# First chunk of a recurrent layer with experts: three sums per job read from the matmul bank by VectorE

## The chip, the cores and the metric

The kernel runs on one core of a Trainium2 chip, as one launch. The metric is the device time of the launch in microseconds. The core has five engines that run side by side and wait for each other by semaphores: TensorE (PE in the profile, its weight loads PEld), VectorE (DVE), ScalarE (ACT), GpSimd (POOL) and SyncE (SP), which issues most of the transfers. [...] The kernel before takes 4155.28 us, the median of three runs (4152.07 to 4155.88).

## What is computed

The input x has 8 x 1024 rows of 512 numbers in float32. The reference, cut to what matters here:

```python
xn = layernorm(x)
# recurrent part, Din = 1024
proj = xn @ W1 + b1
hidden, forget_gate, input_gate = split(proj, 3)
# a gated linear recurrence along the rows, computed with logarithms
out_h = ...
s = out_h @ W2 + b2
# expert part
shared = (silu(xn @ shared_gate_w) * (xn @ shared_up_w)) @ shared_down_w
e = argmax(xn @ gate_w)              # one of 32 experts for each row
xs = xn * sigmoid(max(xn @ gate_w))
routed = (silu(xs @ routed_gate_w[e]) * (xs @ routed_up_w[e])) @ routed_down_w[e]
out = x + s * silu(shared + routed)
```

## The kernel before, in words

The kernel works in two stages. The first makes the recurrent part and the shared expert for 16 chunks of 512 rows; the second (from about 2780 us on) makes the routed experts. The change lies in the first chunk of the first stage.

**Jobs and products.** A chunk has 20 jobs. A job makes one 256-wide slice of one projection: f, i or h (forget, input and hidden part of `proj`, slices 0 to 3) or g or u (gate and up projection of the shared expert). The order is `0fih 1fih 0gu 2fih 1gu 3fih 2gu 3gu` (JOBS, L542). Jobs are numbered on through the chunks, so job 20 is the first one of the second chunk. The first three jobs of the first chunk are plain products (`plain`, L851); all others multiply two 2x2 block matrices with seven products instead of eight, in the form with shared partial sums (`multiply`, L880). Each product P1 to P7 is two matmuls of 128x128 by 128x256. In the trace, in which a float32 matmul shows two records, a product is four records; products that follow each other without a wait start 0.86 us apart.

**Banks.** A job has three accumulators in PSUM. The chain bank b (three buffers) takes P1, P6, P7 and P4 in this order, each adding to what is there; after each of them the bank is read out, and only then may the next one of the chain begin. Bank c takes P5 and then P3 on top of it. Bank a takes P2. In the first chunk bank a is always the single buffer x0 and bank c goes round u0, u1 and x1 (L908). From the second chunk on a and c take turns with x0 and x1 (L906); the first c product of the second chunk, P5 of job 20, takes x0.

**Reading out.** ScalarE copies the bank to a part tile in SBUF, with the bias of the projection where one is due (L931 a plain copy, L933 a copy with a bias; g and u jobs have no bias and use L931 throughout). The part tiles are p1 (of P1), a (P2), p5 (P5), u2 (P6), c (P3) and u3 (P7), each with two buffers; the trace drops the numbers, so p1 and p5 both show as p, and u2 and u3 both as u. Three of the four quarters of the job's output are then sums of two parts: a + p1, c + u2 and u3 + p5 (L943, `join`). They are put into the queue one slot later, on VectorE; from the second chunk on the sum u3 + p5 is made by GpSimd. The fourth quarter is P4's copy itself.

**Order of the work.** The order on each engine is written out by hand in slots (`manual_schedule`; the loop over `now`, L1613). A slot holds one product, so a job has seven slots: P1 of job n, P4 of job n-2, P5 of n, P7 of n-1, P2 of n, P6 of n and P3, in the first chunk of job n-1 (ORDER, L962). Everything else is put down for a slot with `at`: loads of weights, the partial sums of weight blocks (GpSimd L788 to L792, VectorE L794), the partial sums of output weights (GpSimd, 1024 wide, L1123), and per slice the steps of the recurrence (class Cell): Abs, Exp and Ln on ScalarE (L983, L987, L991), a difference and two corrections on VectorE (L995, L999, L1003), sigmoids and Relu on ScalarE (L1006, L1010, L1013), a value and a product on VectorE (L1016, L1019) and two scans of 128x512 on VectorE (L1028). An engine takes its queue strictly in order. From the second chunk on, matmuls of the output projection (L1239) stand between the products.

Of the kernel before, what the change touches and what calls it, by code (L numbers as in the profile page):

```python
# [11 lines left out]
ALU = mybir.AluOpType  # L12
# [22 lines left out]
def tile_kernel(  # L35
# [45 lines left out]
    nc = tc.nc  # L81
# [27 lines left out]
    def work(name):  # L109
# [11 lines left out]
        out=upper, in_=ones, pattern=[[1, P]], compare_op=ALU.is_gt, fill=0.0,  # L121
# [429 lines left out]
    HT = T // 2  # L551
# [21 lines left out]
    now = 0  # L573
    steps = {}

    def at(slot, what, *args):
        assert slot >= now
        steps.setdefault(slot, []).append(lambda: what(*args))
# [194 lines left out]
    def blocks(n):  # L773
        w = natural[n]
        return [w[:, k : k + KQ, m : m + P] for m in (0, P) for k in (0, KQ)]
# [62 lines left out]
    outs, banks = {}, {}  # L838

    def out_of(n):  # L840
        c, q = divmod(n, JC)
        p, kind = JOBS[q]
        outs[n] = jp.tile([P, 2, T], FP, tag="out", name=f"{kind}{c}_{p}", bufs=7)
        return outs[n]

    def bias(n, block):
        p, kind = JOBS[n % JC]
        col = "hfi".index(kind) * NJ + 2 * p + block
        return vec[:, col : col + 1]
# [30 lines left out]
    def multiply(name, n):  # L880

        c = n // JC
        kind = JOBS[n % JC][1]
        A11, A12, A21, A22 = blocks(n)
        S = sums.get(n)
        b = xnTs[c]

        def B(k, m):
            return b[:, k * KQ : (k + 1) * KQ, m * HT : (m + 1) * HT]

        lhs, rhs, bank = {
            "P1": lambda: (A11, B(0, 0), "b"),
            "P2": lambda: (A12, B(1, 0), "a"),
            "P3": lambda: (S[:, 3], B(1, 1), "c"),
            "P4": lambda: (A22, tsum[c, 4], "b"),
            "P5": lambda: (S[:, 0], tsum[c, 1], "c"),
            "P6": lambda: (S[:, 1], tsum[c, 2], "b"),
            "P7": lambda: (S[:, 2], tsum[c, 3], "b"),
        }[name]()
        new = name in ("P1", "P2", "P5")  # L900
        if new:
            if bank == "b":
                ps = ps_b.tile([P, 512], FP, tag="b", name=f"b{n}")
            else:
                if n >= JC:
                    tag = f"x{(n + (bank == 'a')) % 2}"  # L906
                else:
                    tag = "x0" if bank == "a" else ("u0", "u1", "x1")[n % 3]  # L908
                if tag[0] == "u":
                    ps = ps_u.tile([P, 2, HC], FP, tag=tag, name=f"{bank}{n}")  # L910
                    ps = ps.rearrange("p q f -> p (q f)")
                else:
                    ps = ps_x.tile([P, 512], FP, tag=tag, name=f"{bank}{n}")
            banks[n, bank] = ps
        ps = banks[n, bank][:, :HT]
        for k in range(KQ):
            nc.tensor.matmul(  # L917
                ps, lhsT=lhs[:, k, :], rhs=rhs[:, k, :],
                start=(new and k == 0), stop=(k == KQ - 1),

                skip_group_check=True,
            )

        def part(tag, bufs):
            o = jp.tile([P, HT], FP, tag=tag, name=f"{tag}{n}", bufs=bufs)
            outs[n, tag] = o
            return o

        def evict(o, block):
            if block is None or kind in "gu":  # L930
                nc.scalar.copy(o, ps)  # L931
            else:
                nc.scalar.activation(o, ps, AF.Identity, bias=bias(n, block))  # L933

        if name == "P1":
            out_of(n)
            evict(part("p1", 2), 0)
            return
        o = outs[n]

        def join(eng, out, *tags):
            l, r = (outs.pop((n, tag)) for tag in tags)
            at(now + 1, lambda: eng.tensor_tensor(out, l, r, ALU.add))  # L943

        if name == "P2":
            evict(part("a", 2), None)
            join(nc.vector, o[:, 0, :HT], "a", "p1")
        elif name == "P5":
            evict(part("p5", 2), None)
        elif name == "P6":  # L950
            evict(part("u2", 2), 0)
        elif name == "P3":
            evict(part("c", 2), None)
            join(nc.vector, o[:, 0, HT:], "c", "u2")
        elif name == "P7":
            evict(part("u3", 2), 1)
            join(nc.gpsimd if c else nc.vector, o[:, 1, HT:], "u3", "p5")
        elif name == "P4":
            evict(o[:, 1, :HT], 1)
            natural.pop(n)  # L960
# [652 lines left out]
    for now in range(END):  # L1613
        job = now // 7
        name, back = ORDER[now % 7]
        if now < 7 * NPL:
            plain(job, now % 7)
        todo = (job - back,) if name != "P3" else (job - 1, job)
        for n in todo:
            late = name == "P3" and n < JC  # L1620
            if NPL <= n < NJOB and n == job - (1 if late else back):
                multiply(name, n)
        for step in steps.pop(now, ()):
            step()
        while filled < due(now):
            next(fill)
            filled += 1
# [112 lines left out]
    with tc.tile_pool(name="wo", bufs=3) as wo, tc.tile_pool(name="so", bufs=3) as so:  # L1740
        n = nc.values_load(
            nov[0:1, 0:1], min_val=0, max_val=MAXOV,
            skip_runtime_bounds_check_because="a sum of at most MAXOV comparisons of counts that sum to N",
        )
# [59 lines left out]
```

## Time and profile before

| what | value |
|---|---|
| median of three runs | 4155.28 us (4152.07 to 4155.88) |
| the profiled execution | 4155.68 us, its span 4153.9 us |
| mean granted clock of TensorE | 0.997 |
| busy: VectorE, ScalarE, GpSimd | 2257.2, 2113.6, 1391.7 us |
| sums of L943 in the first chunk | 51 on VectorE |
| products of L917 in the first chunk | from 39.25 us on |
| first matmul of the output projection (L1239) | 167.93 us |

The span runs from the first to the last instruction that the profiler saw; the run's time holds a little more. Busy time of an engine is the sum of its instructions. In a timeline a row gives start, duration, engine, line, operation, output<-inputs, and in brackets how long the engine stood idle before and whose work ended that. A wait row names the engine and tile that waited, then what it waited for, then total us, times and the longest.

### The profile page before, as it was taken

How to read it: one execution, taken by the hardware profiler on the slowest of the kernel's cores; microseconds unless marked ns; L12 is line 12 of the kernel's file. 1: busy time of each engine (PE TensorE's matmuls, PEld its weight loads, DVE VectorE, ACT ScalarE, POOL GpSimd, SP SyncE). 2: the span in 40 equal slices, each digit the busy share in tenths (PEclk: the TensorE clock that was granted, in tenths of full speed). 3: DMA queues.
4: the chain of work that ended last, by engine and by line, in shares of the span. 5: the costliest groups of instructions: out<-in, count | busy, mean ns of one | idle time of the engine just before them, and what ended most of it. 6: DMA issues, size and time to landing. Idle time of an engine off the chain costs nothing. (4 is left out here: it accounts for less than half of the span.)

```text
span 4153.9 us, 60141 instructions
## 1 busy us (share of the span) xinstructions
PE 4101.2 (99%) x21515; PEld 3635.9 (88%) x21515; DVE 2257.2 (54%) x3682; ACT 2113.6 (51%) x4031; POOL 1391.7 (34%) x1539
## 2 busy tenths in 40 slices
PE   7999999999999999999999999999999999999997
PEld 5788888888888888888888888887899999999997
DVE  6655555564555645556555566534555656666631
ACT  5666666666766667666676666731222222222210
POOL 5322111221112211212112122634555555555542
PEclk9999999999999999999999999999999999999999
DMA  8766666666666766667666665575777787888884
GB/s 277 238 220 222 208 221 204 217 223 216 216 206 210 228 218 216 211 200 227 220 213 217 203 221 183 183 236 180 212 227 233 219 243 232 247 250 234 245 260 118
DMA packets 557537, 909.30 MB, mean 219 GB/s; under 512 B 55404, under 2 KB 315404, under 8 KB 556980
## 3 DMA queue, kind: packets, MB, share of 16 engines
q1 hardware_dynamic: 510356, 816.23, 60.7%
q0 software_dynamic: 46880, 89.20, 8.8%
q8 instruction: 172, 2.82, 0.3%
q14 instruction: 129, 1.06, 0.1%
HBM read 786.82 MB, written 136.37 MB: 222 GB/s over the span
## 5 line engine op out<-in xcount | busy, mean ns | idle before, releaser
L917 PE MATMUL b<-t,sums 128*128 128x256 f32 x2536 | 653.9, 380 | 14.1 <-ACT u L933 6.5
L1239 PE MATMUL u<-wP,s 128*128 128x256 f32 x2032 | 598.0, 380 | 2.0 <-issue 2.0
L917 PEld LDWEIGHTS b<-t,sums 128*128 128x128 f32 x2536 | 480.8, 190 | 83.9 <-ACT u L933 8.9
L331 PE MATMUL acc<-e_h,e_wd 128*128 128x284 f32 (+26 forms) x2048 | 514.7, 394 | 0.0
L1239 PEld LDWEIGHTS u<-wP,s 128*128 128x128 f32 x2032 | 386.9, 191 | 56.9 <-issue 4.2
L331 PEld LDWEIGHTS acc<-e_h,e_wd 128*128 128x128 f32 x2048 | 373.6, 190 | 64.9
L252 POOL DMA_INDIRECT e_xs<-rec,fours x276 | 300.0, 1087 | 91.4 <-issue 87.7
L917 PE MATMUL b<-t,nat 128*128 128x256 f32 x1268 | 325.9, 379 | 4.6 <-ACT u L931 3.8
L917 PE MATMUL a<-xnT,nat 128*128 128x256 f32 x1268 | 326.8, 380 | 0.0
L917 PE MATMUL b<-xnT,nat 128*128 128x256 f32 x1268 | 325.4, 379 | 0.0
L917 PE MATMUL c<-t,sums 128*128 128x256 f32 x1268 | 325.4, 379 | 0.0
L917 PE MATMUL c<-xnT,sums 128*128 128x256 f32 x1268 | 325.2, 379 | 0.0
L933 ACT ACTIVATE u<-b,vec 128x256 f32<-128x256 f32 x378 | 179.8, 476 | 188.3 <-PE b L917 172.3
L917 PEld LDWEIGHTS b<-t,nat 128*128 128x128 f32 x1268 | 240.5, 190 | 39.1 <-ACT u L931 5.4
L917 PEld LDWEIGHTS a<-xnT,nat 128*128 128x128 f32 x1268 | 241.9, 191 | 33.2
L917 PEld LDWEIGHTS b<-xnT,nat 128*128 128x128 f32 x1268 | 240.9, 190 | 33.2 <-issue 0.5
L917 PEld LDWEIGHTS c<-xnT,sums 128*128 128x128 f32 x1268 | 241.0, 190 | 32.8
L917 PEld LDWEIGHTS c<-t,sums 128*128 128x128 f32 x1268 | 240.9, 190 | 32.8
L1239 PE MATMUL u<-wP,h 128*128 128x256 f32 x768 | 225.1, 379 | 0.0
L995 DVE TENSOR_TENSOR d<-d,m 128x1024 f32<-128x1024 f32 x64 | 87.7, 1370 | 239.8 <-ACT m L991 239.8
L1239 PE MATMUL u<-wP,sh 128*128 128x256 f32 x720 | 215.6, 381 | 0.0
L406 ACT COPY e_s<-e_b 128x284 f32<-128x284 f32 (+21 forms) x216 | 84.4, 391 | 239.8 <-PE e_b L397 239.8
(291 smaller groups left out, 7796.5 us busy)
## 6 DMA issues: line engine op xcount, KB each, us to landing
sums<-sdram SPq DMA_DIRECT2D x300, 512.0 KB, 4.6
nat<-in_L_attn_W_dram SPq DMA_DIRECT2D x192, 512.0 KB, 4.5
e_w<-L_ffn_routed_gate_w_dram SPq DMA_DIRECT2D x128, 512.0 KB, 4.6
e_w<-n_L_ffn_routed_up_w_dram SPq DMA_DIRECT2D x128, 512.0 KB, 8.6
e_wd<-L_ffn_routed_down_w_dram SPq DMA_DIRECT2D x32, 2048.0 KB, 10.9
wP<-tdram SPq DMA_DIRECT2D x127, 512.0 KB, 3.9
nat<-L_ffn_shared_gate_w_dram SPq DMA_DIRECT2D x64, 512.0 KB, 4.6
nat<-n_L_ffn_shared_up_w_dram SPq DMA_DIRECT2D x64, 512.0 KB, 4.2
```

What stands on the lines that cost most here:

```text
L252: nc.gpsimd.indirect_dma_start(out=self.xs[t][:, b, :], out_offset=None, in_=rec1.rearrange("n (a d) -> (n a) d", a=NA), in_offset=bass.In ...
L331: nc.tensor.matmul(accs[m][:, :W], lhsT=self.wd[:, j, m * P : (m + 1) * P], rhs=h[:, :W], start=(j == 0), stop=(j == NI - 1),)
L406: nc.scalar.copy(o[:, :W], ps[:, :W])
L917: nc.tensor.matmul(ps, lhsT=lhs[:, k, :], rhs=rhs[:, k, :], start=(new and k == 0), stop=(k == KQ - 1),  skip_group_check=True,)
L933: nc.scalar.activation(o, ps, AF.Identity, bias=bias(n, block))
L995: nc.vector.tensor_tensor(d, d, self.li, ALU.subtract)
L1239: nc.tensor.matmul(ps[:, q, :], lhsT=lhs[:, q * P : (q + 1) * P], rhs=w[:, p],  start=(q == 0 and p == 0 and name in ("P1", "P2", "P5")), ...
```

## The change

For the first chunk (c == 0) the second, third and seventh product are no longer copied to a part tile by ScalarE. VectorE makes the sum in one instruction, with one input in the bank (`ps`) and the other in the part tile that was there before: p1, u2 or p5. The bias that u3 carried goes into the copy of P5 instead. As before, the sum is put down one slot after its product. The branch for u3 + p5 is on GpSimd in all other chunks, as it was.

```diff
+        def direct(out, tag):
+            r = outs.pop((n, tag))
+            at(now + 1, lambda: nc.vector.tensor_tensor(out, ps, r, ALU.add))
+
-        if name == "P2":
+        if c == 0 and name in ("P2", "P3", "P7"):
+            direct(*{
+                "P2": (o[:, 0, :HT], "p1"), "P3": (o[:, 0, HT:], "u2"), "P7": (o[:, 1, HT:], "p5"),
+            }[name])
+        elif name == "P2":
             evict(part("a", 2), None)
             join(nc.vector, o[:, 0, :HT], "a", "p1")
         elif name == "P5":
-            evict(part("p5", 2), None)
+            evict(part("p5", 2), None if c else 1)
...
         elif name == "P7":
             evict(part("u3", 2), 1)
-            join(nc.gpsimd if c else nc.vector, o[:, 1, HT:], "u3", "p5")
+            join(nc.gpsimd, o[:, 1, HT:], "u3", "p5")
```

## The prediction

> **What bounds the kernel.** I read the busy table first, then the windows, then what TensorE waited for, then the timelines of the stretch with idle time.
>
> ```profile
> PE 4101.2 (99%) x21515; PEld 3635.9 (88%) x21515; DVE 2257.2 (54%) x3682; ACT 2113.6 (51%) x4031; POOL 1391.7 (34%) x1539
> ```
>
> TensorE is busy 4101.2 of 4153.9 us, so whatever makes it wait is paid in full, and what any other engine saves is worth nothing unless TensorE waited for it. The chunk that the change touches runs from 39 to about 165 us. Its windows (stretch, length, busy time of TensorE, weight load, VectorE, ScalarE, GpSimd, granted clock, DMA):
>
> ```profile
> 60.00:70.00 10.00, 9.03 (x43) 7.62 (x42) 10.00 (x9) 9.95 (x17) 10.00 (x9) 1.00 0.90 317
> 70.00:80.00 10.00, 4.50 (x17) 3.28 (x16) 9.93 (x10) 4.99 (x10) 9.43 (x7) 0.91 1.00 369
> 130.00:140.00 10.00, 8.22 (x41) 5.95 (x40) 9.93 (x12) 2.19 (x6) 9.69 (x9) 1.00 0.45 152
> ```
>
> Summed from 40 to 165 us TensorE is idle 17.5 us; from 200 to 2300 us it shows none. So 17.5 us (0.42%) is all that this change can win. Look at the third busy column: VectorE is at 9.9 to 10 of 10 where TensorE idles most. The waits, TensorE's and then ScalarE's, in that stretch (total, times, longest):
>
> ```profile
> PE b L917 <- ACT u L931: 10.2, 7, 4.3
> PE b L917 <- ACT u L933: 7.3, 7, 2.1
> ```
> ```profile
> ACT u L933 <- DVE f L943: 10.4, 2, 5.3
> ACT u L931 <- DVE h L943: 4.6, 1, 4.6
> ```
>
> TensorE waits only for ScalarE's copies out of the chain bank. But three of these waits, TensorE's 4.28, 2.08 and 1.78 us, come after ScalarE itself stood still behind a VectorE sum that had yet to free its buffer. So 8.1 us are VectorE's doing and 9.3 us ScalarE's own queue: copies that stand behind table loads (1.28 us) and 1024-wide activations (1.06 to 1.15 us).
>
> **What is removed.** Jobs 3 to 19, 17 of them, lose three copies each: 51 ScalarE instructions. Copies of a and c show 376 and 374 ns and start 0.26 us apart when queued, biased ones 480 ns and 0.37 us apart. A job loses 0.26+0.26 and 0.26 (g, u) or 0.37 (f, i, h): about 0.83 us, or 14 us over the chunk. All of it lies beside TensorE work except where a copy of the chain bank stands behind it. P5's copy gets a bias for the 9 jobs of f, i, h: 480 against 381 ns, 0.9 us in all, beside other work.
>
> **What is changed on VectorE.** The same 51 sums stand at the same places in its queue (the seventh product's was VectorE's in this chunk already). Only the source changes. No row shows a 256-wide sum out of a bank, so I bound it. A 512-wide one with one input in a bank (L1251) takes 688 ns, and one with both in SBUF (L829) 690 to 699 ns: no extra. So an undisturbed 256-wide one should cost what the undisturbed SBUF one costs, 0.42 us; the other end is today's, 0.94 us where GpSimd works at the same time. These groups show which it will be:
>
> ```profile
> L943 DVE TENSOR_TENSOR f<-a,p 128x256 f32<-128x256 f32 x63 | 39.2, 622 | 120.6 <-ACT a L931 120.6
> L1222 DVE TENSOR_TENSOR a<-u,b2b 128x512 f32<-128x512 f32 x32 | 22.0, 688 | 33.9 <-PE u L1239 33.8
> L1251 DVE TENSOR_TENSOR o<-u,a 128x512 f32<-128x512 f32 x32 | 22.0, 688 | 20.5 <-PE u L1239 15.2 <-DMA rec<-o 5.2
> ```
>
> The 622 ns of the first is a mixture of 0.42 and 0.95; the two with a bank as source keep 688 ns in the mean, also where GpSimd works. I take 0.42 us. From 50 to 140 us that takes some 8 us off the stretched sums, but part comes back, since the next instruction with two SBUF inputs then waits for the same GpSimd instruction.
>
> [...]
>
> **What is added: TensorE now waits for VectorE's queue.** ScalarE used to empty bank a and the chain bank within about a microsecond or two. Now the next P2 needs the sum of this P2 (a single bank x0), P4 needs the P7 sum of its job, and P5 three jobs on needs the P3 sum. Behind the waiting product stands all of TensorE's queue. Where VectorE is late today, two buffers of each part hide it; this cover goes. TensorE, with the products P4, P5 and P7 of jobs 6, 8 and 7, and then VectorE:
>
> ```profile
> 72.46 1.13 PE L917 MATMUL b<-t,nat 128*128 128x256 f32 x4 [1.23 <-ACT u L931]
> 73.42 1.03 PE L917 MATMUL c<-t,sums 128*128 128x256 f32 x4
> 78.73 2.07 PE L917 MATMUL b<-t,sums 128*128 128x256 f32 x4 [4.28 <-ACT u L931]
> ```
> ```profile
> 74.01 3.41 DVE L1028 TENSOR_TENSOR_SCAN h<-i,ginit,f 128x512 f32<-128x512 f32 x1
> ...
> 77.52 0.69 DVE L943 TENSOR_TENSOR h<-c,u 128x256 f32<-128x256 f32 x1
> ...
> 79.00 0.94 DVE L943 TENSOR_TENSOR g<-u,p 128x256 f32<-128x256 f32 x1
> ```
>
> P4 of job 6 starts at 72.46, but the sum that it will need (g<-u,p) ends at 79.94: 7.5 us late. The same subtraction gives 6.0 us for job 9 (97.34 against 103.36) and 7.1 us for job 14 (133.21 against 140.36), and 1.3 to 5.6 us for ten others. These do not add up: VectorE's time sets them, and two products later stands a wait that TensorE has today anyway. With P4 at 80.0, P7 of job 7 follows two products (1.73 us) later at 81.7 and not 78.7: 3.0 us lost, not 7.5. Job 9 gives 103.4+1.7=105.1 against 101.3, 3.8 us; job 14 gives 140.4+1.7=142.1 against 136.9, 5.2 us, all if VectorE is as late as today. The next waits of today (1.18, 0.79 and 1.51 us) then swallow 3.5 us of it.
>
> **The sum is set at the last gate.** P5 of job 20 opens the next chunk, takes bank x0, and so must wait for the sum of job 19's P2. Past it ScalarE copies again, and TensorE has no wait that gives anything back. VectorE, TensorE and ScalarE:
>
> ```profile
> 170.49 0.98 DVE L943 TENSOR_TENSOR u<-a,p 128x256 f32<-128x256 f32 x1
> ```
> ```profile
> 166.21 1.03 PE L917 MATMUL c<-t,sums 128*128 128x256 f32 x4
> ```
> ```profile
> 160.60 1.08 ACT L1013 ACTIVATE h<-h 128x1024 f32<-128x1024 f32 x1
> ```
>
> - Upper end: that sum ends where it does now, 171.47. Then P5 is 171.47-166.21 = 5.3 us late, and 6.6 us if TensorE's lag costs ScalarE another 1.3 us.
> - Middle: VectorE last rests before 161.72, for the ScalarE instruction that ends at 161.68. From there to 171.47 it works without a gap, less 0.56 us for the one stretched sum: 9.2 us. ScalarE is busy from 140.44 up to its end but for 1.57 us (a wait for VectorE, which moves along), and loses eight copies in it, one at 0.37 and seven at 0.26 us, 2.2 us in all. So 161.68-2.2+9.2 = 168.7: P5 is late by 2.5 us. Two or three late P4 before it wake ScalarE late, 0.5 to 1 us: 3 us.
> - Lower end: VectorE also reaches 140 us earlier, by part of the 8 us. At 5 us the gate is open at 163.7 and TensorE, with the ScalarE waits of 9.3 us partly gone and P4's partly come, gains about 2 us.
>
> I take the middle: **4155.7 + 3 = 4158.7 us**. The profiled execution took 4155.68 us (1.8 beside its span of 4153.9), 0.4 above the median 4155.28 of the runs shown. About 0.2%, 8.3 us, is what a measurement of this kernel can tell from no change.
>
> **Rivals.**
> - *ScalarE's relief wins (faster).* The eleven waits that stem from ScalarE's own queue shrink (9.3 us), and sums at 0.42 us let VectorE run ahead, so that the three of 8.1 us shrink too. With two thirds of 17.5 us gone: 4144; the least that counts is 8.3 us. For it: 14 us of copies gone from a queue that TensorE waits for. Against: P6's copy, for which P7 waits 12.9 of the 17.5 us, stays on ScalarE.
> - *VectorE's backlog becomes the bound (slower).* The 8 us come back at the next two-input instructions, GpSimd's 2.3 us sums (L1123) hold the scans as today, and TensorE's lag delays ScalarE and so VectorE. It decides from the point where the sum of job 19's P2 ends after 166.2+8.3 = 174.5, 3 us later than now. Price 8.3 to 12: about 4166. The clock can add: after waits of 4.28 and 2.08 us the granted clock is 0.56 and 0.66 in the next 3.5 and 5 us, so a dip costs 3.5x0.44 = 1.5 to 5x0.34 = 1.7 us.
> - *It doesn't do what it says.* The built order shows 51 ScalarE instructions fewer and VectorE's in the same order; I give this nothing.
>
> [...]
>
> **Chances.** Forecast (within 8.3 us) 0.60, backlog 0.27, relief 0.13. For 8 in 10 the range leaves out the far parts of both rivals: 4148 to 4168. The forecast's own range, from the lower and upper ends, is 4153.5 to 4162.5.
>
> **What would show it.** Right: sums at 0.42 us throughout the chunk; ScalarE's copies of a and c gone before 165 us; TensorE's waits in the chunk for VectorE (L943's new line) on P4 of jobs 6, 9 and 14 at 2 to 5 us and on the first c product of the next chunk; first product of L1239, at 167.93 today, at about 171. Wrong: no TensorE wait for VectorE in the chunk (relief), or sums from a bank at 0.9 us (backlog), or a difference that arises after 200 us.

## The result, and the profile after

| | before | after |
|---|---|---|
| median (lowest to highest), 16 runs each | 4154.66 us (4151.96 to 4156.48) | 4162.09 us (4159.09 to 4166.63) |
| ratio after / before | | 1.0019, 95% interval 1.0012 to 1.0026 |
| the profiled execution, its span | 4155.68, 4153.9 us | 4163.02, 4161.3 us |
| chunk: first L917 product to first output product | 128.68 us | 137.64 us |
| TensorE idle in it | 17.48 us | 18.23 us |
| time at half the granted clock in it | 6.83 us | 27.31 us |

The change costs 7.4 us (0.19%); 4158.7 was forecast, so the sign was right and the size too small. The last three rows are worked out from the trace's records. They carry the explanation: TensorE waits about as long as before in sum, but four times as much time passes at half clock. (The profile records the clock that TensorE was granted; in every profile here it is either full, 1.00, or half, 0.50. A stretch at half clock is called a drop below.) In line numbers of the new kernel the sum from a bank is L947, the output product L1247, and what stood behind L943 has moved down by 8.

Busy time on the page of the new kernel, and the same three windows as before (stretch, length, TensorE, weight load, VectorE, ScalarE, GpSimd, clock, DMA share, GB/s):

```profile
PE 4107.3 (99%) x21515; PEld 3647.2 (88%) x21515; DVE 2248.9 (54%) x3682; ACT 2099.4 (50%) x3980; POOL 1394.9 (34%) x1539
```
```profile
60.00:70.00 10.00, 5.57 (x20) 4.47 (x21) 9.85 (x12) 6.50 (x10) 10.00 (x9) 0.88 0.59 229
70.00:80.00 10.00, 10.00 (x38) 8.42 (x37) 9.42 (x11) 6.14 (x10) 9.43 (x7) 0.78 0.71 243
130.00:140.00 10.00, 6.53 (x24) 5.21 (x23) 9.97 (x14) 1.21 (x3) 9.06 (x9) 0.79 0.37 117
```

ScalarE has 51 instructions and 14.2 us less. TensorE is "busy" 6.1 us more with the same number of matmuls, which is the mark of a slower clock, not of more work. From 70 to 80 us it looks fully busy (10.00), but the clock column shows 0.78: a busy share alone would call this stretch the best of the three.

The longest rows of what TensorE waited for from 40 to 180 us, and ScalarE's first row of waits for VectorE (total, times, longest):

```profile
PE b L917 <- DVE i L947: 6.8, 2, 3.5
PE b L917 <- DVE h L947: 3.0, 1, 3.0
PE b L917 <- DVE g L947: 2.9, 2, 2.2
PE a L917 <- DVE h L947: 1.7, 1, 1.7
PE c L917 <- DVE u L947: 1.6, 1, 1.6
PE b L917 <- ACT u L933: 0.9, 2, 0.8
```
```profile
ACT u L933 <- DVE f L947: 8.0, 2, 4.4
```

The waits for ScalarE, 17.5 us before, are down to 0.9; VectorE's sums have taken their place. Each long one is at P4, which needs the P7 sum of its job out of the chain bank: 3.00 us (job 5), 3.37 (job 9), 3.47 (job 14), 2.23 (job 16). What follows such a wait is seen in TensorE's timeline at P4 of job 5 and of job 14:

```profile
68.16 2.08 PE L917 MATMUL b<-t,nat 128*128 128x256 f32 x4 [3.00 <-DVE h L947]
70.02 1.92 PE L917 MATMUL c<-t,sums 128*128 128x256 f32 x4
```
```profile
137.11 2.08 PE L917 MATMUL b<-t,nat 128*128 128x256 f32 x4 [3.47 <-DVE i L947]
138.98 1.92 PE L917 MATMUL c<-t,sums 128*128 128x256 f32 x4
140.68 1.92 PE L917 MATMUL b<-t,sums 128*128 128x256 f32 x4
142.39 1.15 PE L917 MATMUL a<-xnT,nat 128*128 128x256 f32 x4
143.46 1.07 PE L668 MATMUL lgp<-xnT,gw 128*32 128x512 f32 x8
```

A product of four records takes 1.03 us at full clock; here four of them take 1.92 to 2.08 us and start 1.7 to 1.9 us apart instead of 0.86. The rows carry no mark for this: one sees it only by comparing durations of equal shape. The product of the router's logits (lgp) at the end starts at 143.46 instead of 138.80 us, and with it the rest of the chunk: ScalarE's copy of lgp stands in its queue ahead of the functions that VectorE needs. Before, TensorE's row of lgp and ScalarE's copy were:

```profile
138.80 1.07 PE L668 MATMUL lgp<-xnT,gw 128*32 128x512 f32 x8
```
```profile
142.28 0.61 ACT L673 COPY lgT<-lgp 128x512 f32<-128x512 f32 x1
```

After, ScalarE, then VectorE, then TensorE, to the end of the chunk:

```profile
144.60 0.59 ACT L673 COPY lgT<-lgp 128x512 f32<-128x512 f32 x1 [2.30 <-PE lgp L668]
...
157.93 0.37 ACT L931 COPY g<-b 128x256 f32<-128x256 f32 x1 [3.28 <-PE b L917]
...
163.09 1.06 ACT L1021 ACTIVATE h<-h 128x1024 f32<-128x1024 f32 x1
```
```profile
164.18 1.22 DVE L1024 SCALAR_TENSOR_TENSOR h<-m,h 128x1024 f32<-128x1024 f32 x1 [1.86 <-ACT h L1021]
...
172.95 0.41 DVE L947 TENSOR_TENSOR u<-a,p 128x256 f32<-128x256 f32 x1
```
```profile
173.42 2.07 PE L917 MATMUL c<-t,sums 128*128 128x256 f32 x4 [1.58 <-DVE u L947]
...
176.88 0.60 PE L1247 MATMUL u<-wP,h 128*128 128x256 f32 x2
```

The last gate exists: P5 of job 20 waits 1.58 us for the sum of job 19's P2, starts 7.2 us later than before, and at half clock; the first output product comes 9.0 us later (176.88 against 167.93). From 180 to 2300 us the clock is 1.00 and TensorE is full (2120.00 of 2120 us busy) in both kernels. One half-clock window of before at 2778 us (1.7 us of time) is absent in the profile after: 9.0 - 1.7 = 7.3, which is the difference of the two profiled executions.

### The profile page after: what moved, and what is told of

Same layout as the page of the kernel before. It is cut to its first block, busy times and chain, and to the rows that moved or that the text cites. A ratio compares the mean times of both kernels' runs of the same rounds, so it can differ in the third digit from the quotient of the medians.

```text
span 4161.3 us, 60091 instructions
## 1 busy us (share of the span) xinstructions
PE 4107.3 (99%) x21515; PEld 3647.2 (88%) x21515; DVE 2248.9 (54%) x3682; ACT 2099.4 (50%) x3980; POOL 1394.9 (34%) x1539
## 5 line engine op out<-in xcount | busy, mean ns | idle before, releaser
L917 PE MATMUL b<-t,sums 128*128 128x256 f32 x2536 | 655.2, 381 | 2.1 <-DVE t L829 1.2
L1247 PE MATMUL u<-wP,s 128*128 128x256 f32 x2032 | 596.8, 380 | 2.2 <-issue 2.2
L917 PEld LDWEIGHTS b<-t,sums 128*128 128x128 f32 x2536 | 484.1, 191 | 69.1 <-ACT u L933 1.8
L1247 PEld LDWEIGHTS u<-wP,s 128*128 128x128 f32 x2032 | 386.6, 190 | 55.7 <-issue 4.5
L917 PE MATMUL b<-t,nat 128*128 128x256 f32 x1268 | 329.9, 383 | 13.5 <-DVE i L947 6.8
L917 PE MATMUL c<-t,sums 128*128 128x256 f32 x1268 | 330.2, 384 | 1.6 <-DVE u L947 1.6
L917 PE MATMUL a<-xnT,nat 128*128 128x256 f32 x1268 | 326.5, 380 | 1.7 <-DVE h L947 1.7
L917 PE MATMUL b<-xnT,nat 128*128 128x256 f32 x1268 | 325.7, 379 | 0.4 <-DMA nat<-L_ffn_shared_gate_w_dram 0.4
L917 PE MATMUL c<-xnT,sums 128*128 128x256 f32 x1268 | 325.4, 379 | 0.0
L917 PEld LDWEIGHTS b<-t,nat 128*128 128x128 f32 x1268 | 242.7, 192 | 48.7 <-DVE i L947 7.6
L917 PEld LDWEIGHTS c<-t,sums 128*128 128x128 f32 x1268 | 244.2, 193 | 35.3 <-DVE u L947 2.0
L917 PEld LDWEIGHTS a<-xnT,nat 128*128 128x128 f32 x1268 | 242.3, 191 | 34.8 <-DVE h L947 2.1
L917 PEld LDWEIGHTS b<-xnT,nat 128*128 128x128 f32 x1268 | 241.4, 190 | 33.4 <-issue 1.3
L917 PEld LDWEIGHTS c<-xnT,sums 128*128 128x128 f32 x1268 | 241.4, 190 | 32.2
L1247 PE MATMUL u<-wP,h 128*128 128x256 f32 x768 | 225.4, 379 | 0.0
L1247 PE MATMUL u<-wP,sh 128*128 128x256 f32 x720 | 215.8, 381 | 0.0
```

Of the source, the lines that this page charges most:

```text
L917: nc.tensor.matmul(ps, lhsT=lhs[:, k, :], rhs=rhs[:, k, :], start=(new and k == 0), stop=(k == KQ - 1),  skip_group_check=True,)
L1247: nc.tensor.matmul(ps[:, q, :], lhsT=lhs[:, q * P : (q + 1) * P], rhs=w[:, p],  start=(q == 0 and p == 0 and name in ("P1", "P2", "P5")), ...
```

## The experiments

Three theories were put to the test. **A**: the sums that free the chain bank (P7) make TensorE wait for VectorE's queue, and that is the loss. **B**: not the waits cost, which sum up as before, but the half clock behind the long ones. **C**: the gate at the end of the chunk, where a bank passes to the next stage, sets the time. Each kernel's ratio is to the kernel before on the same chip in the same session (its median 4154.0 to 4154.8 us). "Up to lgp" is the time from the first L917 product to the logits' product (99.55 us before, 104.23 after), "from lgp" that from there to the first output product (29.13 and 33.41).

### One part at a time

P7 back on ScalarE, P2 and P3 direct:

```diff
-        if c == 0 and name in ("P2", "P3", "P7"):
+        if c == 0 and name in ("P2", "P3"):
...
-            evict(part("p5", 2), None if c else 1)
+            evict(part("p5", 2), None)
...
-            join(nc.gpsimd, o[:, 1, HT:], "u3", "p5")
+            join(nc.gpsimd if c else nc.vector, o[:, 1, HT:], "u3", "p5")
```

> The second and third product are still summed from the bank; the seventh goes back to ScalarE's copy and the sum of two part tiles, and P5's copy loses its bias again. Theory A (the chain bank is the gate: P4 waits for the P7 sum in VectorE's queue): the five waits of P4 for VectorE (3.0, 3.4, 0.7, 3.5, 2.2 us) and the half-clock stretches behind them go; 4151 to 4157 us, no slower than the kernel before. Theory C (the last gate sets the time: P5 of job 20 in bank x0 waits for the sum of P2 of job 19): this gate stays and VectorE's queue is as long, so 4159 to 4162.

Measured: 4158.2 us, ratio 1.0007 (0.9998 to 1.0016). Up to lgp 99.20 us, as before; from lgp 33.97, as after. The time lies between the two forecasts. About half of the loss goes with P7, as A says, and the profile shows the other half at the end of the chunk; the interval of what is left just reaches no change.

Only P7 direct:

```diff
+        if c == 0 and name == "P7":
```

> Only the seventh product is summed from the bank; second and third are copied by ScalarE as in the kernel before. Theory A: P4 waits for VectorE as in the changed kernel, 4159 to 4164 us. Theory C: the gate of bank x0 is gone with P2's sum, so 4153 to 4157.

Measured: 4165.9 us, 1.0027 (1.0017 to 1.0037): by the medians worse than all three together, though the intervals overlap. Its waits at P4 are 4.6, 3.6 and 4.8 us, up to lgp it takes 108.68 us, and from there 29.49, without a loss. Its rows of sums, the first two from SBUF, the third from the bank, say why:

```profile
L943 DVE TENSOR_TENSOR g<-a,p 128x256 f32<-128x256 f32 x4 | 3.6, 894 | 1.2 <-ACT a L931 1.2
...
L943 DVE TENSOR_TENSOR i<-a,p 128x256 f32<-128x256 f32 x3 | 1.8, 607 | 4.8 <-ACT a L931 4.8
...
L947 DVE TENSOR_TENSOR g<-b,p 128x256 f32<-128x256 f32 x4 | 1.7, 415 | 0.0
```

The other sums are stretched as before, so VectorE should reach the P7 sum later: it seems that the direct P2 and P3 sums help the third one to be on time.

Only P3 direct, and only P2 direct (the same line with `name == "P3"` and `name == "P2"`; P7 and P5 as in the kernel before):

> Only the third product is summed from the bank. Its bank comes round three jobs later, so its gate seldom closes. Theory A (the gate on a bank that is needed soon, with the half clock behind it, is the cost): no wait of TensorE for VectorE over 2 us, and ScalarE has 17 copies less: 4150 to 4156 us. If VectorE reading a bank is the cost as such: about a third of the change, 4156 to 4158.

Measured: 4161.15 us, 1.0016 (1.0007 to 1.0025). A miss for A. Up to lgp it is 98.27 us, but from lgp 34.52, and TensorE's timeline shows where:

```profile
166.07 1.03 PE L917 MATMUL b<-t,sums 128*128 128x256 f32 x4
172.85 1.22 PE L1247 MATMUL u<-wP,h 128*128 128x256 f32 x2 [5.75 <-DVE g L947]
```

The output projection's first product takes over bank u0, and in u0 stands the c sum of job 18, which VectorE now empties. A second gate at the end, that the prediction had not seen.

> Only the second product is summed from the bank. Theory A: P2 of the next job waits for VectorE where it is late, above all job 7 (about 4.8 us, as with P2 and P3 together) and P5 of job 20 (4.3 us), with half clock behind both: 4156 to 4161 us. If the third product's sum made the loss of the run with P2 and P3 together: 4153 to 4156.

Measured: 4159.7 us, 1.0011 (1.0002 to 1.0020). Up to lgp 99.55 us, to the digit that of before, although P2 of job 7 waits 4.82 us in it and a drop of 6.8 us follows, so that the equality to the digit is chance; from lgp 33.60, with a wait of 4.31 us at P5 of job 20. What P2 alone costs shows at x0, at the end of the chunk.

### The clock

The new kernel with five matmuls that feed nothing, ahead of P4 of jobs 5, 9 and 14:

```diff
+                if name == "P4" and n in (5, 9, 14):
+                    idle = work(f"idle{n}")
+                    for _ in range(5):
+                        nc.tensor.matmul(
+                            idle[:, :HT], lhsT=ident, rhs=xnTs[0][:, 0, :HT], start=True, stop=True
+                        )
```

> The changed kernel with five matmuls more (128x128 by 128x256, result never read) ahead of P4 of jobs 5, 9 and 14, 2.2 us each time, in waits of 3.0, 3.4 and 3.5 us. Theory B (the waits themselves cost no more than before, the half clock behind the longer ones does): the three half-clock stretches of 6.8 us behind these waits go, and the time falls by 2 to 6 us to 4156 to 4160 though TensorE does more. If only the waits count: no change, 4161 to 4164, for the added work lies in the waits.

Measured: 4157.64 us, 1.0007 (0.9998 to 1.0016): 6.5 us of additional TensorE work make the kernel 4.5 us faster than the new kernel, and the slowest of its 11 runs (4159.09) is level with the fastest of the new kernel's 16. TensorE at P4 of job 5, and the window from 60 to 80 us (clock 0.83 in the kernel after):

```profile
64.99 2.32 PE L1633 MATMUL idle<-xnT,ident 128*128 128x256 f32 x10
68.16 1.13 PE L917 MATMUL b<-t,nat 128*128 128x256 f32 x4 [0.84 <-DVE h L947]
69.12 1.03 PE L917 MATMUL c<-t,sums 128*128 128x256 f32 x4
```
```profile
60.00:80.00 20.00, 17.59 (x79) 14.88 (x80) 19.78 (x22) 13.78 (x20) 19.77 (x15) 1.00 0.75 266
```

P4 starts at 68.16 us in both kernels, since VectorE sets that; but behind it the products take 1.03 us and not 1.92. B holds: up to lgp 99.12 us instead of 104.23.

The same in the kernel before, five ahead of P7 of job 7 and two ahead of P7 of job 10:

> The kernel before with five idle matmuls ahead of P7 of job 7 and two ahead of P7 of job 10 (waits of 4.28 and 2.08 us, each with 3.4 us of half clock behind it). Theory B: both half-clock stretches go, 1.7 us each, of which later waits of ScalarE's and VectorE's may swallow some: 1 to 3 us less than before, 4151 to 4153.5. If the half clock is no cost here: 4154 to 4156, as the kernel before.

Measured: 4154.61 us, 1.0000 (0.9991 to 1.0009). A miss: no gain. The two drops of the clock went, but a wait of 2.9 us arose at 88 us, with a drop of its own.

Where do the drops come from? In all fourteen profiles the edges of the half-clock times stand on a grid of 3.413 us (in the profile before, half-clock times begin at 78.186 and 2778.128 us, and the 2699.942 us between them are 791 steps of 3.4133). Counted over the chunk (in the one profile without a drop there, the grid is read from the half-clock time at the end of the kernel): every full-clock grid window with 2.02 us or more of TensorE idle time is followed by one at half clock (34 of 34), and none with 1.71 us or less; of the seven in between, 1.72 to 1.84 us, one is. A half-clock window with 0.63 us idle or more is followed by another (10 of 10), one with 0.58 us or less is not. So the place of a wait in the grid should count, not its length alone. Two and four such matmuls ahead of job 3, the first one with seven products, shift all waits against the grid:

```diff
+                if name == "P1" and n == 3:
+                    idle = work(f"idle{n}")
+                    for _ in range(2):
```

> The changed kernel with two idle matmuls (0.87 us) ahead of the chunk's first job, so that all its waits come 0.87 us later in the program. In every profile so far the drops of the clock stand on a grid of 3.413 us that is nearly fixed against the start of the program, and a grid window with 2.02 us or more of TensorE idle time is followed by one at half rate, one with 1.74 us or less is not. Theory 'the grid': the waits of 3.0, 3.4, 2.2 and 1.6 us are now cut in two by a window's edge, their windows hold 1.5 to 1.65 us each, and only the wait at P4 of job 14 keeps a drop: half-clock time falls from 27.3 to 3.4-7 us, 10 to 12 us of time at half rate less 0.9 us; since the grid moves by some 0.5 us from one execution to the next, the median should gain part of it: 4153 to 4158.5 us. Theory 'a long wait brings its drop wherever it stands': the same drops and 0.9 us more, 4163 us (4161 to 4165).

Measured: 4159.84 us, 1.0014 (1.0005 to 1.0023). TensorE at P4 of job 5, the same wait as after:

```profile
68.88 1.13 PE L917 MATMUL b<-t,nat 128*128 128x256 f32 x4 [3.01 <-DVE h L947]
69.84 1.03 PE L917 MATMUL c<-t,sums 128*128 128x256 f32 x4
```

A wait of 3.01 us, cut by an edge into 1.36 and 1.64, and no drop. The half-clock time in the chunk is 6.83 us instead of 27.31, as the grid says; but the time lies between the two forecasts of this run, outside both. Idle time rose from 18.23 to 21.92 us: part of what the slow clock had taken would have been waited for VectorE anyway.

> The changed kernel with four idle matmuls (1.73 us) ahead of the chunk's first job. Theory 'the grid': windows at P4 of jobs 5, 9 and 14 hold 2.35 to 3.0 us of idle time and little follows in the next, so each brings one drop of 3.4 us and not 6.8, and those at 156 and 173 us go: 10.2 us at half rate in place of 27.3, 8.5 us less, and 1.7 us more work: 4155.3 us (4154 to 4159), more than with two idle matmuls. Theory 'a long wait brings its drop wherever it stands': 4163.8 us (4162 to 4166).

Measured: 4160.68 us, 1.0017 (1.0008 to 1.0026). Five drops of 3.41 us, 17.06 in all: the three at P4 are single as forecast, the two at the end did not go, and the time is again outside both forecasts. The edges themselves lay up to 1.7 us apart against the chunk's start from one execution to the next, which is half a window; a shift of the program does not control them.

### The last gate

From the second chunk on, banks x0 and x1 exchanged, with P7 direct and with P7 back:

```diff
-                    tag = f"x{(n + (bank == 'a')) % 2}"
+                    tag = f"x{(n + (bank != 'a')) % 2}"
```

> The changed kernel with the banks x0 and x1 exchanged from the second chunk on, so that P5 of job 20 takes x1 and need not wait for the sum of P2 of job 19. Theory C: the wait of 1.6 us and the half clock of 3.4 us behind it go, 3.3 us less: 4158 to 4159.5. If VectorE's lateness is merely met at another place (P2 of job 20 in x0, four slots and the first matmuls of the output projection later): 4160 to 4163.

Measured: 4160.78 us, 1.0014 (1.0005 to 1.0023).

> Second and third product from the bank, the seventh by ScalarE, and the banks x0 and x1 exchanged from the second chunk on. Of the run without the exchange (4158.2) the last gate took 4.3 us and two half-clock stretches (6.8 us, 3.4 lost). P2 of job 20 meets the same sum some 3.5 us later, so 2 to 5 us less: 4153 to 4156. If the gate is merely met later at its full price: 4157 to 4159.

Measured: 4159.39 us, 1.0015 (1.0006 to 1.0024), a miss. In both the wait at P5 of job 20 is gone, and the first output product waits instead, 2.4 and 5.2 us, for the sum in u0. Opening one gate only brought the other to light.

Both gates at once: jobs 17 to 19 are copied by ScalarE as before, all others stay direct. Then the same with the fillers:

```diff
-        if c == 0 and name in ("P2", "P3", "P7"):
+        if n < 17 and name in ("P2", "P3", "P7"):
...
-            evict(part("p5", 2), None if c else 1)
+            evict(part("p5", 2), 1 if n < 17 else None)
...
-            join(nc.gpsimd, o[:, 1, HT:], "u3", "p5")
+            join(nc.gpsimd if c else nc.vector, o[:, 1, HT:], "u3", "p5")
```

> The changed kernel, but the last three jobs of the chunk (17, 18, 19) have their a, c and u3 copied out by ScalarE again, so no bank that the next chunk or the output projection takes over waits for VectorE. Theory 'the end gate costs': the wait of 1.58 us at P5 of job 20 goes, with the half clock behind it (3.4 us at half rate, 1.7 us): 3.3 us less than the changed kernel, about 4158.8 us (4157 to 4160.5), first output-projection matmul at about 173.5. Theory 'VectorE's lag costs, whatever bank shows it': ScalarE's nine copies stand in its queue again, the first output product waits elsewhere, and the time stays at 4160.5 to 4163. If only the clock counts, it depends on the dip at 173.4 alone: with a wait under 1.8 us in its place, 1.7 us less, 4160.4.

Measured: 4154.6 us, 1.0000 (0.9991 to 1.0009): level with before, 7.5 us below after and below all three forecasts, so C gains more than it expected. The cleanest comparison is with the run with four shifting matmuls, because VectorE is equally far in both. There (VectorE, then TensorE):

```profile
170.96 0.42 DVE L947 TENSOR_TENSOR u<-a,p 128x256 f32<-128x256 f32 x1
```
```profile
171.43 1.56 PE L917 MATMUL c<-t,sums 128*128 128x256 f32 x4 [1.58 <-DVE u L947]
172.78 1.91 PE L917 MATMUL b<-t,sums 128*128 128x256 f32 x4
174.49 1.05 PE L1247 MATMUL u<-wP,h 128*128 128x256 f32 x2
```

Here:

```profile
171.11 0.98 DVE L943 TENSOR_TENSOR u<-a,p 128x256 f32<-128x256 f32 x1
```
```profile
167.43 1.03 PE L917 MATMUL c<-t,sums 128*128 128x256 f32 x4
168.29 1.03 PE L917 MATMUL b<-t,sums 128*128 128x256 f32 x4
169.16 0.59 PE L1247 MATMUL u<-wP,h 128*128 128x256 f32 x2
```

The same sum starts at 170.96 and 171.11 us. In the one kernel TensorE stands until it is done; in the other it has started the output projection 1.95 us before that sum begins. The logits' product is at 141.79 and 141.82 us, the output product at 174.49 and 169.16: 5.3 us for the gates of the last three jobs and the slow clock around them. Up to lgp the two profiles of the same program (this one and after, which differ only from job 17 on) are 102.41 and 104.23 us long; these 1.8 us are the grid, whose drops are 3.4 us here and 6.8 there.

> The same as the run with the last three jobs copied by ScalarE, and five idle matmuls ahead of P4 of jobs 5, 9 and 14 as in the run with fillers. If the two effects add (4.5 us of half clock behind the chain bank's gates, 3.3 us at the end of the chunk): 4162.1 - 4.5 - 3.3 = 4154.3 us, level with the kernel before (4152 to 4156.5). If the end of the chunk is set by VectorE's chain to the last job and not by TensorE's arrivals, the fillers' gain is waited away there: 4157 to 4159, as the run with fillers alone.

Measured: 4152.27 us, 0.9995 (0.9986 to 1.0004). The two remedies go together, but not in full: 9.8 us below after, where they gave 4.5 and 7.5 us singly. There is no drop of the clock in the chunk, and up to lgp and from lgp take 98.50 and 27.34 us, each shorter than before. Beside the kernel before it is 2.55 us lower, which the interval does not tell from no change.

## Why the prediction was near, and where it failed

The measured 4162.09 us lies in the stated 4148 to 4168, and at the upper end of the forecast's own 4153.5 to 4162.5. That end was drawn for another course (the last sum ending at 171.47 us as before, and 1.3 us of lag), so to lie just inside it is partly luck. The prediction also held 8.3 us for the least that a measurement can tell from no change; with 16 runs the interval of 1.0012 to 1.0026 tells 7.4 us from none.

- **Winnable time.** TensorE's idle time in the chunk was the right account, and none of it was won: 17.48 and 18.23 us. That it was the *whole* account was wrong, as the clock is a second one.
- **Copies removed.** 14 us forecast, less 0.9 us for P5's bias; ScalarE's busy time fell by 14.2 us.
- **Sums at 0.42 us.** Right throughout. Three rows of the sums from a bank (lowest/median/highest ns, first and last start):

```profile
L947 DVE TENSOR_TENSOR u<-a,p x4: 412/420/425, 75.0 to 172.9; 128x256 f32<-128x256 f32 x4
...
L947 DVE TENSOR_TENSOR h<-b,p x3: 411/424/425, 67.7 to 142.7; 128x256 f32<-128x256 f32 x3
...
L947 DVE TENSOR_TENSOR h<-c,u x3: 416/425/425, 73.4 to 146.5; 128x256 f32<-128x256 f32 x3
```

  GpSimd is busy 10.00 of 10 us from 60 to 70 us and none is stretched, while the SBUF sums of the runs with one part take up to 0.95 us there. In the profile before, the 20 sums of two part tiles that take 0.61 to 0.97 us (40 to 165 us) all end 0.28 or 0.29 us after the end of a GpSimd instruction that runs beside them; after, the 25 sums from a bank that run beside one take 408 to 425 ns.
- **P4 waits for VectorE.** Right in kind and size: 3.00, 3.37 and 3.47 us, where 2 to 5 us was the sign given (the 3.0, 3.8 and 5.2 us beside it were losses of TensorE against before, not waits); job 5 instead of 6, and job 16 beside them. That they don't add up to a loss of idle time was right too: 13.78 us idle up to lgp after, 14.01 before.
- **The last gate.** Its middle estimate had three parts, and the numbers of two hold almost to the digit, the first by luck. ScalarE's gain between lgp and the instruction that wakes VectorE: 2.2 forecast for eight copies; 22.88 us before and 20.69 after, 2.19. But all of it lies ahead of the copy of lgp, which starts 3.48 us after lgp before and 1.14 us after the change: ScalarE had stood behind VectorE until 140.44 us and had copies ahead of it. From that copy to the end of the waking instruction it takes 19.40 and 19.55 us. Six copies fewer lie in there, but ScalarE waits 3.28 us for P4 of job 16 (157.93 us), where it waited 1.57 us for VectorE before. VectorE's gapless work from the waking instruction to the end of the last sum: 9.2 forecast, 9.18 measured (164.18 to 173.36). The third failed: "Two or three late P4 before it wake ScalarE late, 0.5 to 1 us". It was **4.66 us** (lgp at 143.46 instead of 138.80).
- **Why that step failed.** It priced the waits, whose sum stayed the same, and not what stands behind them. Half-clock time up to lgp rose from 6.83 to 20.48 us; TensorE worked in 6.3 and 17.4 us of it, and half of the difference, 5.6 us, less 0.2 us idle, is the 4.66 but for 0.7, which stays open. The prediction had this price, 1.5 to 1.7 us per drop, but put it with the slower rival and not into the forecast, though its own P4 losses of 3.0 to 5.2 us lay above the 2.08 us that it had seen suffice.
- **Sum.** 4.66 (lgp late) + 2.5 (the gate as forecast) + 1.7 (half clock behind the last gate) = 8.9 of the chunk's 9.0 us, less 1.7 us at 2778 us. Forecast 3. That the drop at 2778 us is absent after is, as the author reads it, chance of the grid and no gain of the change: before, a wait of 1.96 us lies there in one grid window, after, one of 2.18 us is cut by an edge into 0.56 and 1.62.
- **The rivals.** ScalarE's relief was real but TensorE did not wait for it any longer. VectorE's backlog did not bind as described: the last sum ended at 173.36 us, before the 174.5 that were given as its point. That P3's banks were left out ("within about a microsecond or two" was said of a and b) was a gap: u0 is the second gate.
- **What stays open.** Why the drop at 2778 us comes in some profiles and not in others was not tried; the idle time there lies at the edge (a grid window with 1.96 us brought it, one with 1.98 us did not). How far the grid's place differs over the other executions is not known either: each kernel has one profile. The run with P3 alone loses 5.4 us from lgp on, and how that divides between wait and clock was not separated.

## What to carry to other kernels

Before the reader of an accumulator bank is changed, list who takes the bank over next, the last banks of a stage above all: a direct sum by an engine with a long queue is worth taking in the middle of the stage and is best left to the idle engine for the last few jobs. Count an engine's waits by length and place and not by their sum: a few waits above 2 us can cost TensorE a second time in clock, which shows as equal shapes that take twice as long (1.92 to 2.08 us here instead of 1.03). If nothing better fills such a wait, a few idle matmuls can; in the kernel before they won nothing, as another wait arose.

## What the runs showed of the hardware

- Equal idle time, unequal time: 17.5 and 18.2 us idle in the chunk, but 6.8 and 27.3 us at half clock.
- 6.5 us of useless matmuls made the new kernel 4.5 us faster.
- The clock follows a grid of 3.413 us: in the chunk, 2.02 us idle or more within one window brought the next one to half clock (34 of 34), 1.71 us or less never did; once there, 0.63 us idle or more kept it there for another window (10 of 10). A wait of 3.01 us that an edge cut in two had no drop behind it.
- Time won back from the clock is not all won: in the run with two shifting matmuls 20.5 us less at half clock, worth 10.2 us at most, made the chunk 4.2 us shorter; 3.7 us of more waiting are the largest part of the rest.
